# A two-layer conv and state-space network on one core: a cubic softplus with its bias in the product, and conv kernels composed before the branch

## The chip, the cores and the metric

The kernel runs on one core of a Trainium2 chip. A core has five engines with a queue of instructions each: TensorE (PE in the profile, with its weight loads as PEld), VectorE (DVE), ScalarE (ACT), GpSimd (POOL) and SyncE (SP), which here issues nearly all DMAs. The engines meet only at semaphores, and each works through its queue in order. The metric is the device time of one execution in microseconds (us). Before the change, three runs gave a median of 1218.54 us (1215.86 to 1219.69).

## The reference

The input is one image of 64 x 64 positions with 96 channels. It goes through two layers; each is a mixer and an MLP, both with a norm in front and a residual sum behind. All is float32 but the MLPs, which round to 8-bit floats.

Layer 0's mixer projects to 192 channels and a gate, applies a 3x3 convolution per channel, and runs a scan over the 4096 positions in four directions. Layer 1's mixer has a full 3x3 convolution over 192 channels and again scans with a state of 16 per channel. Both make their step sizes with a softplus:

```python
x_dbl = u @ x_proj_w                       # 192 -> 6 + 16 + 16
dt = jax.nn.softplus(dt @ dt_proj_w + dt_proj_b)
...
def step(h, inp):                          # layer 1's scan, per position
    u_t, dt_t, B_t, C_t = inp
    dA = jnp.exp(dt_t[..., None] * A)
    h = dA * h + (dt_t * u_t)[..., None] * B_t[:, None, :]
    y = jnp.sum(h * C_t[:, None, :], axis=-1)
```

## The kernel before

**Stages.** There are four. The *front* (layer 0) is written out by hand: norm and projection, the conv per channel on TensorE, and scans over the ends of the sequences alone (`scan_ends`), since the states fade. A bit computed from the data (`alive`) decides whether the full scan is needed (`tc.If` at line 318, in `layer0`); with these inputs it isn't, and every engine branches past it. The *middle* does layer 0's mix and MLP, the norm of layer 1, its conv and the projections to step sizes and states. The *scans* of layer 1 are 24 passes over 4096 positions (lines 1966 to 2042). The *tail* is layer 1's output projection and MLP.

**What sets the order.** The front keeps the order of its code: `keep` pins an instruction behind all that its engine was given before. In the middle a planner (`Order`) chooses: `o.add(engine, cost, ...)` gives an operation with the tiles that it reads and writes and an estimated cost; `run` always takes an operation that can start first, and among these the one with the longest chain behind it plus a lead from the table `LEAD`. What comes out is the fixed order of each engine's queue. DMAs of `open1` (weights of layer 1) are issued before all that the planner places on SP, and the planner does not count them.

**Softplus.** With z = sigmoid(-|x| - ln 2), softplus(x) is max(x, 0) plus z times a polynomial in z squared. Layer 0 (`dt_proj` and `log1p` in `scan_ends`, lines 736 to 756) works on three tiles of 128 x 320: on ScalarE Abs and Relu, both with dt's bias, then Sigmoid and Square; on VectorE `polynomial` (lines 990 to 997), six operations. Layer 1 (`softplus` in `project`, lines 1704 to 1723) works on 12 tiles of 128 x 512, three for each of the four units (0,0), (0,1), (4,0), (4,1): five operations on ScalarE (lines 1714, 1716, 1717, 1719, 1720) and five on VectorE (1715, 1718, 1721, 1722, 1723), which exchange values twice.

**Layer 1's conv kernels.** The projection into the conv is linear, so its weights and the conv's are multiplied into one kernel from 96 channels (`compose1`, lines 1294 to 1352, part of the middle's plan): 2 transposes, 5 steps of products with 2 taps each (line 1329), a halved copy of each on ScalarE (1332), copies of the outer taps on VectorE (1338), and three sums on GpSimd (1350). `open1` loads its inputs (lines 1258 and 1261, 1.3 MB) right after the branch, then 13 small pieces of weights (lines 1281 to 1290).

**The middle's chain.** For each of four pairs of chunks, `mix0` forms means on TensorE (1366, 1370), subtracts them on VectorE (1374, 1378), squares on ScalarE (1381), gates on GpSimd (1385), sums squares (1401), takes the root (1407) and turns it by two small DMAs on SP into a factor per token, `r` (`by_token`, line 1411). VectorE inverts `r` (1415) and adds the mixer's output to the residual (1445). Then come `mlp0` for each chunk, a norm, and images for the conv (1551). `conv_unit` makes 12 products per unit (1584, 1586) and `project` the states and step sizes (1650 to 1780). The last unit, (4,1), ends with 12 products that copy rows to four partitions each (1807), and the first decays and scans start from those.

## Time and profile before

| | |
|---|---|
| time of the profiled execution | 1217.9 us |
| its span | 1216.1 us |
| front | 0 to 102.2 us |
| middle | 102.5 to about 303 us |
| scans | about 303 to 1118 us |
| busy share: VectorE, TensorE, ScalarE, GpSimd | 93%, 84%, 74%, 69% |
| TensorE's clock at its lowest | 0.50 of full, in 99 to 105 us and 270 to 325 us |

A line of the timeline has the start, the duration, the engine, the line of the kernel, the operation with the tiles that it writes and reads, a count where neighbours are merged, and in brackets how long the engine sat idle before it and what released it. SPq, DVEq and so on are an engine's sequencer, which also issues the DMAs. A line of windows has the stretch, its length, busy time and number of instructions of PE, PEld, DVE, ACT and POOL, the granted clock of TensorE, the DMA engines' share and GB/s.

### The profile page before, as it was taken

The page shows a single profiled execution, that of the slowest core. Times are in us where ns is not written, and L with a number is a line of the kernel's source. Part 1 is how long each engine was busy: PE and PEld are TensorE (multiplying, and loading weights), DVE is VectorE, ACT ScalarE, POOL GpSimd, SP SyncE. Part 2 cuts the span into 40 slices and gives each one's busy share as a digit, 9 for nine tenths or more (in the row PEclk, how much of TensorE's full clock was granted, in tenths as well). Part 3 has the DMA queues.
Part 4 walks back from the last instruction along what each step waited for, and adds up shares of the span by engine and source line. Part 5 has one row for each costly group of instructions (what it writes and reads, how often), then busy time and mean ns, then how long its engine had stood idle before and what let it go on. Part 6 is the DMA issues. An engine that isn't in the chain of part 4 may idle for free.

```text
span 1216.1 us, 11204 instructions
## 1 busy us (share of the span) xinstructions
PE 1017.9 (84%) x3488; PEld 414.6 (34%) x3488; DVE 1129.2 (93%) x908; ACT 905.4 (74%) x1177; POOL 841.6 (69%) x510
## 2 busy tenths in 40 slices
PE   9998889985278877888888877898778898899886
PEld 5533333321023322222332322233224443344344
DVE  7895887688898999999999999999999999999978
ACT  5683654656578888887888878888888888898626
POOL 3002464352678888888798788988898887887756
PEclk9998999985589788798878788888789999888987
DMA  2262011376764583575734685545747767343301
GB/s 77 64 180 52 7 21 32 116 254 187 238 192 132 171 250 128 174 229 175 240 99 137 203 251 181 180 131 176 240 129 208 221 194 265 97 143 93 104 1 52
DMA packets 79128, 183.10 MB, mean 151 GB/s; under 512 B 21534, under 2 KB 34936, under 8 KB 77688
## 3 DMA queue, kind: packets, MB, share of 16 engines
q1 hardware_dynamic: 78376, 182.16, 48.2%
q8 instruction: 28, 0.46, 0.2%
q10 hardware_dynamic: 688, 0.19, 0.1%
q14 instruction: 36, 0.29, 0.1%
HBM read 159.73 MB, written 21.52 MB: 149 GB/s over the span
## 4 chain that ended last, share of the span: by engine, by line
DVE 37%; PE 19%; issue 8%; ACT 7%; DMA 3%; POOL 1%; SPq 0%; DVEq 0%; POOLq 0%; ACTq 0%
DVE xws L2014 12%; PE hs L2025 10%; DVE h1s L2014 10%; DVE h0s L2014 8%; PE hs L2029 4%; ACT da L1987 3%; DVE x2s L2014 3%; ACT xws L1972 2%; DVE x1s L2014 2%; DVE x0s L2014 2%; DMA kept<-xn 2%; DMA x2s<-bc 1%; PE acc L2053 1%; PE da L2343 1%; POOL hss L2019 1%
## 5 line engine op out<-in xcount | busy, mean ns | idle before, releaser
L2042 POOL TENSOR_TENSOR kept<-kept,kept 128x1024 f32<-128x1024 f32 x92 | 217.1, 2359 | 83.8 <-issue 45.0
L2019 POOL TENSOR_TENSOR hss<-h1s,xws 128x1024 f32<-128x1024 f32 x96 | 228.0, 2377 | 48.7 <-DVE xws L2014 47.1
L2025 PE MATMUL hs<-h0s,ident 128*128 128x512 f32 x360 | 224.8, 711 | 29.2 <-DVE h0s L2014 24.6
L1987 ACT ACTIVATE da<-dt1s,a 128x1024 f32<-128x1024 f32 x168 | 187.4, 1116 | 58.0 <-DVE xws L2014 49.0
L2014 DVE TENSOR_TENSOR_SCAN xws<-da,xws 128x1024 f32<-128x1024 f32 x96 | 221.5, 2307 | 7.3 <-ACT da L1987 7.2
L1987 ACT ACTIVATE da<-dt0s,a 128x1024 f32<-128x1024 f32 x166 | 185.2, 1115 | 27.2 <-DVE h0s L2014 10.0
L2029 PE MATMUL hs<-hss,ident 128*128 128x512 f32 x368 | 187.8, 602 | 8.1 <-POOL hss L2019 7.9
L2014 DVE TENSOR_TENSOR_SCAN h1s<-da,xws 128x1024 f32<-128x1024 f32 x69 | 156.0, 2261 | 0.0
L2053 PE MATMUL acc<-kept,fold 128*32 128x512 f32 x368 | 87.0, 683 | 71.8 <-POOL kept L2042 71.8
L2038 ACT COPY kept<-hs 128x512 f32<-128x512 f32 x184 | 107.7, 585 | 43.7 <-PE hs L2029 43.5
L2025 PEld LDWEIGHTS hs<-h0s,ident 128*128 128x128 f32 x360 | 72.4, 219 | 155.2 <-issue 82.4
L2029 PEld LDWEIGHTS hs<-hss,ident 128*128 128x128 f32 x368 | 70.3, 194 | 107.8 <-issue 79.4
L2025 PE MATMUL hs<-x1s,ident 128*128 128x512 f32 x128 | 75.7, 676 | 12.6 <-DVE x1s L2014 12.6
L2025 PE MATMUL hs<-x0s,ident 128*128 128x512 f32 x128 | 74.2, 664 | 13.5 <-DVE x0s L2014 13.5
L2025 PE MATMUL hs<-x2s,ident 128*128 128x512 f32 x120 | 72.9, 693 | 12.1 <-DVE x2s L2014 12.1
L1966 POOL TENSOR_TENSOR x1s<-x1s,dus 128x1024 f32<-128x1024 f32 x32 | 75.6, 2366 | 8.8 <-DMA x1s<-bc 8.8
L1966 POOL TENSOR_TENSOR x2s<-x2s,dus 128x1024 f32<-128x1024 f32 x32 | 75.7, 2366 | 1.3 <-DMA x2s<-bc 1.2
L2014 DVE TENSOR_TENSOR_SCAN x0s<-da,x0s 128x1024 f32<-128x1024 f32 x32 | 73.5, 2296 | 1.3 <-ACT da L1987 1.2
L2014 DVE TENSOR_TENSOR_SCAN x1s<-da,x1s 128x1024 f32<-128x1024 f32 x32 | 73.4, 2293 | 1.3 <-ACT da L1987 1.3
L2014 DVE TENSOR_TENSOR_SCAN x2s<-da,x2s 128x1024 f32<-128x1024 f32 x32 | 73.5, 2298 | 1.0 <-ACT da L1987 0.9
L1972 ACT COPY xws<-x1s 128x1024 f32<-128x1024 f32 x32 | 63.0, 1970 | 5.2 <-POOL hss L2019 5.2
L1966 POOL TENSOR_TENSOR x0s<-x0s,dus 128x1024 f32<-128x1024 f32 x28 | 66.3, 2367 | 0.0
(379 smaller groups left out, 1913.3 us busy)
## 6 DMA issues: line engine op xcount, KB each, us to landing
kept<-bc SPq DMA_DIRECT2D x92, 512.0 KB
x2s<-bc SPq DMA_DIRECT2D x32, 512.0 KB
x0s<-bc SPq DMA_DIRECT2D x28, 512.0 KB
x1s<-bc SPq DMA_DIRECT2D x28, 512.0 KB
dus<-du SPq DMA_DIRECT2D x20, 512.0 KB
dt1s<-dt SPq DMA_DIRECT2D x20, 512.0 KB
dt0s<-dt SPq DMA_DIRECT2D x20, 512.0 KB
kept<-xn SPq DMA_DIRECT2D x24, 384.0 KB
```

The costliest lines, as they stand in the source:

```text
L1966: keep(nc.gpsimd.tensor_tensor(x, x, du[:, part[j]], ALU.mult))
L1972: keep(copy(grid(xw)[:, w, :], cols(xs[i % 3])[:, w, :]))
L1987: keep(nc.scalar.activation(t, dts[o][:, part[j]], AF.Exp, scale=self.a6[:, g, k : k + 1]))
L2014: keep(nc.vector.tensor_tensor_scan(to, da, x, start, ALU.mult, ALU.add))
L2019: keep(nc.gpsimd.tensor_tensor(cols(hs)[:, w, :], grid(h1)[:, w, :], grid(xw)[:, w, :], ALU.add))
L2025: keep(nc.tensor.matmul(t, self.ident, x[:, chunk(m)], start=k == 0, stop=False))
L2029: keep(nc.tensor.matmul(sums[i, m], self.ident, hs[:, chunk(m)], start=False, stop=True))
L2038: keep(nc.scalar.copy(to, sums.pop((i, j * (SC // CH) + h))))
L2042: keep(nc.gpsimd.tensor_tensor(t, t, times_c_by(i, a), ALU.mult))
L2053: keep(nc.tensor.matmul(to, self.fold4, src, start=k == 0, stop=k == NK - 1))
L2343: keep(nc.tensor.matmul(o[:, j], y[r, 2 * k + j : CH : 4], w[r], start=first and j == 0, stop=end and j == 1))
```

## The change

Layer 0's and layer 1's polynomials get one degree less in z squared and a form with one Square on ScalarE. In layer 0 the Relu goes from ScalarE to VectorE. In layer 1 the bias becomes a seventh row of the product: the row of ones comes from an Identity with the bias column `unit`, and the weights get a row loaded by one more DMA per rank block. max(x, 0) and the last sum become one operation.

`compose1` leaves the plan. Its inputs are loaded late in `scan_ends` into tiles that are free by then (`fetch`); its products stand where 19 warming products stood, around the two products `yc`; all of its copies are on ScalarE; the three sums on GpSimd follow, and the result goes to DRAM (`cw_d`, 864 KB). All of this comes before the branch. The middle loads `cw_d` into the conv's tile by one DMA, the first that the planner puts on SP. The planner's costs and leads have new values throughout. The options `BIAS0_POOL` and `NORM0_ACT` are empty and change nothing.

```diff
-RANKS = (slice(0, RANK), slice(96, 96 + RANK))
+RANKS = (slice(0, RANK + 1), slice(96, 96 + RANK + 1))
...
+CUBIC = (0.34226051, 1.83304455, -0.33816952, 3.07350780)
+QS = math.sqrt(CUBIC[0])
+QB = CUBIC[0] * CUBIC[3]
...
-LEAD = {"compose": -84.0}
-LEAD |= {("mix", s): t for s, t in enumerate((1589.0, 1847.0, -1582.0, -1562.0))}
-LEAD |= {("mlp", s): t for s, t in enumerate((1510.0, 80.0, 777.0, -2488.0))}
+LEAD = {"compose": 371.0}
+LEAD |= {("mix", s): t for s, t in enumerate((858.0, 2656.0, -2207.0, -2187.0))}
+LEAD |= {("mlp", s): t for s, t in enumerate((1277.0, 862.0, 1968.0, -5402.0))}
...
+        self.unit = self.column("unit", 0.0)
+        for r in RANKS:
+            nc.gpsimd.tensor_tensor(self.unit, self.unit, self.ident[:, r.stop - 1 : r.stop], ALU.add)
...
             keep(nc.scalar.activation(z[:, s, :], t, AF.Abs, bias=bias))
-            keep(nc.scalar.activation(dt[:, s, :], t, AF.Relu, bias=bias))
+            keep(nc.vector.tensor_scalar(dt[:, s, :], t, bias, 0.0, ALU.add, ALU.max))
             keep(nc.scalar.activation(z[:, s, :], z[:, s, :], AF.Sigmoid, bias=self.nln2, scale=-1.0))
             keep(nc.scalar.activation(zz[:, s, :], z[:, s, :], AF.Square))
+            keep(nc.scalar.activation(p[:, s, :], zz[:, s, :], AF.Square, bias=self.qa, scale=QS))
...
-            self.polynomial(z[:, s, :], zz[:, s, :], dt[:, s, :], p[:, s, :], keep)
+            self.cubic(z[:, s, :], zz[:, s, :], p[:, s, :], keep)
+            keep(nc.vector.tensor_tensor(dt[:, s, :], dt[:, s, :], p[:, s, :], ALU.add))
...
         keep(nc.vector.tensor_tensor(v, v, bc[1], ALU.mult))
+        fetch(*(t.rearrange("p s t -> p (s t)") for t in (w, bc[1])))
...
+        turn()
         others(2)
-        for _ in range(14):
-            keep(nc.tensor.matmul(warm[:, 0:P], self.ident, self.ident, start=True, stop=True))
+        for i in range(0, 4, 2):
+            step(i)
         yc = [pm.tile([P, TE], F32, tag="m", name=f"yc{w}") for w in range(2)]
         for t, r in zip(yc, LANES):
             keep(nc.tensor.matmul(t, self.dup[r], x[r, 5], start=True, stop=True))
-        for _ in range(5):
-            keep(nc.tensor.matmul(warm[:, 0:P], self.ident, self.ident, start=True, stop=True))
+        for i in range(4, 9, 2):
+            step(i)
+        halves()
...
+    def cubic(self, z, zz, p, keep):
+        keep(nc.vector.scalar_tensor_tensor(p, p, QB, z, ALU.add, ALU.mult))
+        keep(nc.vector.scalar_tensor_tensor(p, zz, CUBIC[1], p, ALU.add, ALU.mult))
...
-            nc.sync.dma_start(self.w_dt1[r], w["w_dt"])
+            nc.sync.dma_start(self.w_dt1[r.start : r.start + RANK], w["w_dt"])
+            nc.sync.dma_start(self.w_dt1[r.stop - 1 : r.stop], w["vec"][:, 1:2].rearrange("d o -> o d"))
...
+        def fetch(room, rest):
+            half = rest[0:CD, 0 : 9 * DI].rearrange("p (t o) -> p t o", t=9)
+            for k in range(2):
+                t = room[0 : GP[k], 9 * DI * k : 9 * DI * (k + 1)].rearrange("p (t o) -> p t o", t=9)
+                keep(nc.sync.dma_start(t, w["conv_w"][k * P : k * P + GP[k], :, 0:DI]))
...
+        def step(i):
+            for k in range(2):
+                keep(nc.tensor.matmul(view, turned[0 : GP[k], k], raw[k][:, i : i + n], start=k == 0, stop=k == 1))
+            keep(nc.scalar.activation(half[:, i : i + n], view, AF.Copy, scale=0.5))
+            for j in range(n):
+                y, x = divmod(i + j, 3)
+                if x != 1:
+                    keep(nc.scalar.copy(cwf[:, 3 * x // 2, y], view[:, j]))
+
+        def sums():
+            v = half.rearrange("p (y x) o -> p x y o", x=3)
+            keep(nc.gpsimd.tensor_tensor(v[:, 0], v[:, 0], v[:, 2], ALU.add))
+            keep(nc.gpsimd.tensor_tensor(cwf[:, 1], v[:, 0], v[:, 1], ALU.add))
+            keep(nc.gpsimd.tensor_tensor(cwf[:, 2], v[:, 0], v[:, 1], ALU.subtract))
+            keep(nc.sync.dma_start(self.cw_d, cwf.rearrange("p k y o -> p (k y o)")))
...
+    def spread1(self):
+        o.add("PE", 0.4, lambda: keep(nc.tensor.matmul(at["turn"][0:GC, 0:P], self.fold4, self.ident, start=True, stop=True)), new={"turn": "bank"})
+        o.add("DVE", 0.2, lambda: keep(nc.vector.tensor_copy(self.spread4, at["turn"][0:GC, 0:P])), r=["turn"], w=["spread4"])
+        o.add("SP", 0.65, lambda: keep(nc.sync.dma_start(self.cw1.rearrange("p k y o -> p (k y o)"), self.cw_d)), w=["cw"], kb=885)
...
-            return lambda: keep(nc.scalar.copy(at[xd][:, k], at["x", n, k][0:XE]))
+            return lambda: keep(nc.scalar.activation(at[xd][:, k], at["x", n, k][0:XE], AF.Identity, bias=self.unit[0:XE]))
...
-            o.add("ACT", 0.68, lambda: keep(act(vz(), at[t], AF.Abs, bias=bias)), r=[t], new={w: "w1" if g and not last else "w"}, w=[z])
-            o.add("DVE", 0.73, lambda: keep(dve.tensor_scalar(d(), at[t], bias, 0.0, ALU.add, ALU.max)), r=[t, hold], w=[kd])
+            o.add("ACT", 0.6, lambda: keep(act(vz(), at[t], AF.Abs)), r=[t], new={w: "w1" if g and not last else "w"}, w=[z])
             o.add("ACT", 0.7, lambda: keep(act(vz(), vz(), AF.Sigmoid, bias=self.nln2, scale=-1.0)), r=[w], w=[z], table="sigmoid")
             o.add("ACT", 0.6, lambda: keep(act(vzz(), vz(), AF.Square)), r=[z, w], w=[zz])
-            o.add("DVE", 0.42, lambda: keep(dve.tensor_scalar(p(), vzz(), QC, QD, ALU.mult, ALU.add)), r=[zz, w, hold_u], w=[ku])
-            o.add("ACT", 0.7, lambda: keep(act(vzz(), vzz(), AF.Square, bias=self.qa)), r=[w], w=[zz])
-            o.add("ACT", 0.7, lambda: keep(act(vzz(), vzz(), AF.Square, bias=self.qb)), r=[w], w=[zz])
-            o.add("DVE", 0.69, lambda: keep(dve.scalar_tensor_tensor(p(), vzz(), LOG1P[4], p(), ALU.mult, ALU.add)), r=[zz, w, hold_u], w=[ku])
-            o.add("DVE", 0.69, lambda: keep(dve.tensor_tensor(p(), p(), vz(), ALU.mult)), r=[z, w, hold_u], w=[ku])
-            o.add("DVE", 0.69, lambda: keep(dve.tensor_tensor(d(), d(), p(), ALU.add)), r=[ku, hold, hold_u], w=[kd])
+            o.add("ACT", 0.7, lambda: keep(act(p(), vzz(), AF.Square, bias=self.qa, scale=QS)), r=[zz, w, hold_u], w=[ku])
+            o.add("DVE", 0.63, lambda: keep(dve.scalar_tensor_tensor(p(), p(), QB, vz(), ALU.add, ALU.mult)), r=[z, w, hold_u], w=[ku])
+            o.add("DVE", 0.63, lambda: keep(dve.scalar_tensor_tensor(p(), vzz(), CUBIC[1], p(), ALU.add, ALU.mult)), r=[zz, w, hold_u], w=[ku])
+            o.add("DVE", 0.63, lambda: keep(dve.scalar_tensor_tensor(d(), at[t], 0.0, p(), ALU.max, ALU.add)), r=[t, ku, hold, hold_u], w=[kd])
```

## The prediction

> **What bounds the kernel now.** I read the page first, then the windows by stage, then each queue's timeline from 55 to 330 us, since every edit lies there. The page gives the size of the whole.
>
> ```profile
> span 1216.1 us, 11204 instructions
> PE 1017.9 (84%) x3488; PEld 414.6 (34%) x3488; DVE 1129.2 (93%) x908; ACT 905.4 (74%) x1177; POOL 841.6 (69%) x510
> ```
>
> VectorE's 93% is an average. The windows show one stage that is VectorE's and a middle that isn't.
>
> ```profile
> 140.00:160.00 20.00, 13.30 (x65) 4.66 (x63) 18.81 (x29) 9.52 (x19) 14.71 (x17) 0.83 0.06 10
> 220.00:240.00 20.00, 20.00 (x59) 6.69 (x60) 14.80 (x24) 15.35 (x27) 5.84 (x5) 0.91 0.20 67
> 600.00:800.00 200.00, 163.42 (x403) 58.17 (x401) 199.14 (x91) 166.64 (x193) 172.22 (x78) 0.82 0.55 172
> ```
>
> In the scans VectorE is busy 199 of 200 us, with scans that the change doesn't touch: those 800 us stay. In the middle VectorE leads up to about 165 us (18.8 of 20 at 140, TensorE 13.3), then TensorE (20 of 20 at 220, VectorE 14.8), and from 263 us a chain. So the gain or loss is when the first scan starts (302.7 us now). The crossing from front to middle decides much of it; here are TensorE, SP and GpSimd, with GpSimd's three composing sums.
>
> ```profile
> 92.62 3.39 PE L863 MATMUL warm<-ident 128*128 128x128 f32 x28
> 98.54 0.78 PE L866 MATMUL yc<-bce,dup 64*128 64x160 f32 x4 [2.52 <-issue]
> 102.50 4.41 PE L1366 MATMUL bank<-y,mean 128*128 128x512 f32 x6 [0.75 <-DVEq L318]
> ```
>
> ```profile
> 90.25 0.60 SPq L1878 DMA_DIRECT2D a<-a_log  x1
> 102.96 1.40 SPq L1261 DMA_DIRECT2D raw<-conv_w  x2
> ...
> 113.20 0.83 SPq L1290 DMA_DIRECT2D kept<-vec  x2
> 116.87 1.18 SPq L1411 DMA_DIRECT2D r<-diag  x2
> ```
>
> ```profile
> 102.64 0.31 POOL L1254 MEMSET pairs<- 96x256 f32 x1 [83.21 <-DVEq L318]
> ...
> 138.19 1.40 POOL L1350 TENSOR_TENSOR half<-half 96x576 f32<-96x576 f32 x1
> ...
> 140.73 1.50 POOL L1350 TENSOR_TENSOR cw<-half 96x576 f32<-96x576 f32 x1
> ```
>
> SP has nothing to do from 91 to 102 us and is done with the weights at 114, 3 us before `r` needs it (116.87). GpSimd sits idle for 83 us before the branch. VectorE's queue shows what `r` releases, and the end of the middle.
>
> ```profile
> 119.61 0.20 DVE L1415 RECIPROCAL r<-r 128x8 f32<-128x8 f32 x1 [4.11 <-DMA r<-diag]
> 120.45 1.89 DVE L1445 SCALAR_TENSOR_TENSOR res<-bank,r,res 128x96 f32<-128x96 f32 x8 [0.64 <-PE bank L1436]
> ...
> 267.33 2.28 DVE L1620 TENSOR_TENSOR kept<-kept,kept 128x1024 f32<-128x1024 f32 x1
> ...
> 281.71 0.75 DVE L1718 TENSOR_SCALAR kept<-h1s 128x512 f32<-128x512 f32 x2
> ...
> 286.56 1.28 DVE L1723 TENSOR_TENSOR kept<-kept,kept 128x512 f32<-128x512 f32 x2
> ```
>
> **The change, part by part.** The sum is made against the profiled execution's 1217.9 us (span 1216.1 and 1.8 around it), 0.6 us under the median of 1218.54.
>
> *Layer 0's softplus.* VectorE's chain per tile is 0.32 + 1.54 + 0.49 + 0.49 = 2.84 us; after it is three operations of 0.49 and one from PSUM of about 0.5, 2.0 us. ScalarE changes a Relu (0.52) for a Square (0.47 without a bias). With the last Square at 55.3 us, VectorE reaches the scans of line 795 about 2.3 us sooner. But line 829 needs ScalarE's sigmoid of 816, which stands behind the SiLUs of 634, and these waited for TensorE's conv until 65.08 (5.85 us idle). ScalarE is free at 66.96 and then waited only 0.32 us for VectorE. So 2 of the 2.3 us turn into a new idle of VectorE before 829, and the front's end moves by **-0.3**.
>
> *Composing at the front's end.* `fetch` can start at 80.6 us, when line 830 is done; 1.3 MB took the stretch 103 to 109 before, so it has landed by 88, and the first step is at about 93. ScalarE is free from 93.5 us (5 halvings of 0.49, 6 copies of about 0.36, turned copies): nothing on the path, because VectorE works alone from 93 to 102; without that cover it would be 4.5 us. Three of five steps stand behind `yc`: 98.2 + 0.45 + 1.7 + 1.7 + 1.0 (line 1329's rows) = 103.1, instead of warming products until 101.7. The means then start some 1.5 us later. Now their first six rows take 4.41 us at half clock (0.50 in 99 to 105 us) where two rows later take 1.10, so warm ones win 1.1 to 1.4 back: 0 for the means. Steps at half clock would take 1.43 times (4.41 against 3 x 1.03), 1.9 us more. Row 866 shows that 2.5 us of idle was enough; a gap of 2.24 us before 158.7 was not (1.00 in 155 to 160 us); the new gap is about 1.8 us, between no row. GpSimd: 103.1 + 0.4 for the last halving + 1.40 + 1.50 + 1.44 + hops = 108.1, or 110.0 half-clocked; I take 109. It is still in time for its gating, first at 110.83. The two operations on `unit` (about 0.2 us each at 1 us) hide in the 2.38 us that GpSimd waits for `w_in` at 4 us, and would cost 0.4 otherwise.
>
> The Trainium skill, "TensorE: Matmul & The Clock Gate", Part 1: The HAM clock gate, has the clock halve after an idle window of about 3.4 us. By it the steps run at full clock and the sums end at 108.1, 0.9 earlier than I take; this trace differs, as 2.5 us sufficed.
>
> *SP, the queue that all of this is moved past.* The store of `cw_d` waits for GpSimd's last sum. Behind it in program order stand, on SP: eight `a_log` pieces (85.62 to 90.85, 5.2 us; issued early now because nothing holds them), the branch and its events (94.7 to 95.8, 1.1 us), 15 weight pieces (13 took 6.6 us of issuing within 9.6 us; 7.6 now), the load of `cw_d` (0.65), and only then `r` (2.74 us from issue to line 1415). 109 + 0.7 + 5.2 + 1.1 + 7.6 + 0.65 + 2.74 = 127.0. Two waits have no row: whether the branch waits for landings (0 to the 1.6 us that `r` needs after its second issue) and how far `r` stands behind 864 KB (0 to 2.6 us at the 336 GB/s of 105 to 108 us). Half of each gives 129.1, 9.5 later than 119.61; 0.64 of that was slack (TensorE's wait before 1445): **+8.8**. Low end: `a_log` stays ahead and nothing waits, 108.1 + 0.7 + 1.1 + 7.6 + 0.65 + 2.74 = 120.9: +0.6. High end: 110.0, both waits in full and the old gaps between the weights (3.0 more): 135.2, +15.0. I take the middle since the `a_log` pieces are pinned behind the store. VectorE (1415, 1445, all of the MLPs) waits.
>
> The Trainium skill, "DMA: Bandwidth & Descriptors", Queues, rings and completion order, says that each DMA engine consumes descriptors in ring order. By it `r` waits out the whole load, 1.3 us more than I take; no row of before shows a small transfer behind a large one.
>
> *VectorE's run from `r` to the upper half's images* (120.45 to 163.8 us). Gone: copies of 1338 (1.93 us); idle for the second `r` (0.91), for line 1332 (1.42) and 1329 (0.31); and the stretching of 1528 and 1534 (1.31 and 1.66 us, elsewhere 0.34 and 0.52) beside GpSimd's sums, of which I count 1.4 of 2.1. **-6.0**; between the copies alone, -2, and all 5.2 us of idle with copies and stretching, -9.2.
>
> *TensorE's run, 167.4 to 263.6 us.* The conv and the products keep their rows (a seventh row of a product adds none). What the later mixes still did there (2.9 us of 1422 and 1436) can come earlier, as 7.8 us of composing is gone before it: **-1.5**, between 0 and -2.9.
>
> *Layer 1's softplus.* VectorE's 12 chains fall from 40.5 us (8.9, 6.6, 8.8 and 16.2 by line) to 36 x 0.69 = 24.8, ScalarE's by 8.5. While TensorE leads, that is hidden. On the path is the last unit: 278.07 to 287.84 becomes about 278.07 + 4.3 + 3.7 = 286.1, of which I count -1.5; lines 1715 and 1718 of the last narrow tile, 0.74 + 0.42 = -1.2 in a VectorE that is full from 284 us on; and line 1620, ready at 265.2 but started at 267.33 behind the previous unit's chain, -1.2 of 2.1. Identity for Copy adds 2 x 0.1. Sum **-3.7**, between -1.2 and -4.8. Next late is TensorE's row of copies at half clock.
>
> Sum: -0.3 + 8.8 - 6.0 - 1.5 - 3.7 = -2.7, so **1215.2 us**. All best ends give 1201, all worst 1230.
>
> **The rivals.** *`r` comes in time*: SP is free before the sums matter. For it: the scheduler filled SP's free time before the branch in this trace. Against: the store's pin. With +0.6 for +8.8: 1207.0. *SP's queue in full*: +15.0, the other terms kept, 1221.4. For it: SP's old gaps. Against: the raw load that went with those gaps is gone. *The lower half's images come late*: the last MLP pair has the lowest lead of all (-5402). The last images now end at 214.2 us while TensorE still has the upper half's work; if its three units (about 12 us each) and the rest run out first, TensorE idles until the images are there. It decides from when the last images end some 3 us after that work; 10 us, a little more than the idle of 143 to 163 us (7.4), costs 10: 1225.2. For it: VectorE's late start. Against: VectorE has 15 us less to do.
>
> **How the numbers follow.** About 0.3% (3.7 us) can be told from no change. My forecast holds 0.42 (its own range 1211 to 1220: 0.19 faster, 0.21 same, 0.02 slower), `r` in time 0.22 (0.21, 0.01, 0), SP in full 0.16 (0, 0.09, 0.07), late images 0.20 (0, 0.02, 0.18). Faster 0.40, same 0.33, slower 0.27. The range 1204 to 1227 leaves out the outer parts of the first and last cases.
>
> **What would show it.** Idle of about 1.5 us before line 829's operation; GpSimd's sums ending at 108 to 110 us, the store right after, the weights on SP past 120 us; the first reciprocal of `r` at 129 us with a long wait on its DMA; no idle longer than 1 us on VectorE in the 30 us behind it; TensorE full until some 260 us; the first scan at about 300 us. I'm wrong if `r` comes before 123 or after 134 us, or if TensorE runs dry between the two halves.

## The result, and the profile after

The changed kernel takes 1224.96 us (median of 16 runs, 1217.47 to 1229.17) against 1216.72 us for the kernel before in the same comparison (16 runs): a ratio of 1.0069, with a 95% interval of 1.0054 to 1.0085. It is 8.2 us slower by the medians, 8.4 by the ratio. The profiled execution took 1226.85 us, with a span of 1224.9 us. The prediction said 1215.2 us, a little faster.

The page and the windows of the changed kernel, and then two windows of the kernel before for comparison (stretch, its length, busy time and instructions of PE, PEld, DVE, ACT, POOL, granted clock, DMA share, GB/s):

```profile
span 1224.9 us, 11101 instructions
PE 1024.6 (84%) x3450; PEld 412.5 (34%) x3450; DVE 1107.9 (90%) x870; ACT 900.1 (73%) x1173; POOL 843.8 (69%) x512
```

```profile
40.00:60.00 20.00, 17.53 (x149) 7.22 (x148) 9.45 (x24) 11.52 (x26) 0.00 (x0) 0.74 0.21 58
100.00:120.00 20.00, 19.63 (x32) 5.69 (x30) 7.81 (x22) 5.29 (x15) 0.00 (x0) 0.50 0.00 1
140.00:160.00 20.00, 16.21 (x60) 6.58 (x59) 13.85 (x45) 9.35 (x20) 4.43 (x6) 0.83 0.16 39
220.00:240.00 20.00, 20.00 (x49) 6.84 (x48) 7.72 (x12) 9.14 (x15) 3.31 (x5) 0.91 0.32 95
600.00:800.00 200.00, 162.50 (x417) 58.00 (x415) 199.44 (x91) 166.95 (x198) 173.09 (x78) 0.88 0.55 180
```

```profile
40.00:60.00 20.00, 19.56 (x213) 8.65 (x211) 15.68 (x37) 13.80 (x29) 0.00 (x0) 1.00 0.30 85
100.00:120.00 20.00, 17.98 (x49) 5.92 (x48) 8.05 (x23) 7.73 (x11) 8.31 (x11) 0.86 0.36 78
```

VectorE's work fell by 21 us (1129.2 to 1107.9), and the time rose. The scans are as full as before (199.4 of 200). What is new are two stretches of half clock on TensorE: the second half of 40 to 60 us (0.74 on average over the 20 us, 1.00 before), and all of 100 to 120 us (0.50, 0.86 before). Here is how it came to that, on TensorE, ScalarE and SP of the changed kernel (timeline lines as before):

```profile
50.33 0.82 PE L734 MATMUL xe<-ue,wx 128*80 128x160 f32 x2 [2.47 <-DVE dte L752]
...
97.56 1.97 PE L669 MATMUL z<-xt,w_in 96*64 96x512 f32 x4 [2.47 <-ACT pad L671]
99.46 3.78 PE L666 MATMUL z<-xt,w_in 96*128 96x512 f32 x4
...
105.08 5.52 PE L1332 MATMUL compose<-w,turned 128*96 128x384 f32 x7
...
120.77 4.87 PE L1366 MATMUL bank<-y,mean 128*128 128x512 f32 x6 [1.14 <-ACTq L320]
```

```profile
93.98 3.04 ACT L681 ACTIVATE y<-y,d 128x2048 f32<-128x2048 f32 x2 [2.15 <-DMA u<-y]
```

```profile
81.96 1.41 SPq L1316 DMA_DIRECT2D w<-conv_w  x2
84.52 6.98 SPq L638 DMA_DIRECT2D u<-y  x8
...
124.33 0.34 SPq L1344 DMA_DIRECT2D cw<-cwf  x1
129.99 0.37 SPq L1287 DMA_DIRECT2D kept<-w_x  x1
...
138.54 0.42 SPq L1354 DMA_DIRECT2D cw<-cw  x1
139.08 4.23 SPq L1411 DMA_DIRECT2D r<-pad  x4
```

In the kernel before, the same scaling on ScalarE (there line 679) waited 0.23 us, and not for a DMA:

```profile
86.12 3.04 ACT L679 ACTIVATE y<-y,d 128x2048 f32<-128x2048 f32 x2 [0.23 <-ACT pad L669]
```

Read them from the top. At 50 us TensorE waits for line 752, which is layer 0's max(x, 0), now on VectorE, and behind that wait its granted clock is 0.50 until 60 us. At 82 us SP issues the 1.3 MB of conv weights, and behind them the stores of `u`. ScalarE scales `y` in place (line 681), so it must wait until those stores have read `y`: 2.15 us. Its gate copies (671) hang on that, TensorE waits 2.47 us for them, and from there its products take twice as long (96*128 from 1.91 to 3.78 us for four). The composing starts at 105 us and runs at half clock, and TensorE's first mean of the middle starts at 120.77 us instead of 102.50. GpSimd and VectorE show what follows:

```profile
120.08 1.40 POOL L1341 TENSOR_TENSOR bce<-bce 96x576 f32<-96x576 f32 x1 [100.99 <-ACT bce L1333]
...
122.91 1.40 POOL L1343 TENSOR_TENSOR cwf<-bce 96x576 f32<-96x576 f32 x1
129.77 0.31 POOL L1267 MEMSET pairs<- 96x256 f32 x1 [5.46 <-SPq L320]
```

```profile
49.73 0.55 DVE L752 TENSOR_SCALAR dte<-de,vec 128x320 f32<-128x320 f32 x1
...
111.81 1.51 DVE L887 TENSOR_TENSOR y<-y,yc 64x64 f32<-64x64 f32 x8 [5.14 <-PE yc L872]
126.78 1.28 DVE L1374 TENSOR_TENSOR y<-y,bank 128x512 f32<-128x512 f32 x2 [13.45 <-PE bank L1370]
...
145.20 0.20 DVE L1415 RECIPROCAL r<-r 128x8 f32<-128x8 f32 x1 [12.89 <-DMA r<-pad]
...
309.50 2.27 DVE L2021 TENSOR_TENSOR_SCAN h1s<-da,xws 128x1024 f32<-128x1024 f32 x1
```

The sums end at 124.3 us (forecast 109), `r` is inverted at 145.20 us (forecast 129.1; before 119.61), and the first scan starts at 309.50 us (before 302.72). The account of the two profiled executions has three terms: TensorE's first mean comes 18.3 us later; from there to the first scan it takes 188.7 us instead of 200.2, so 11.5 us less; and from the first scan to the end 2.0 us more. Together +8.8 us, the difference of the spans. The last term is no cause that these runs can tell: with the same scans, that stretch lay between 911 and 917 us in all profiles here but one (925), so single executions scatter by a few us there, and the medians decide.

### The profile page after: what moved, and what is told of

Read it like the earlier page. It is cut to its first block, busy times and chain, and to the rows that moved or that the text cites. A ratio compares the mean times of both kernels' runs of the same rounds, so it can differ in the third digit from the quotient of the medians.

```text
span 1224.9 us, 11101 instructions
## 1 busy us (share of the span) xinstructions
PE 1024.6 (84%) x3450; PEld 412.5 (34%) x3450; DVE 1107.9 (90%) x870; ACT 900.1 (73%) x1173; POOL 843.8 (69%) x512
## 4 chain that ended last, share of the span: by engine, by line
DVE 37%; PE 14%; ACT 8%; issue 8%; DMA 3%; POOL 2%; SPq 0%; DVEq 0%; POOLq 0%; ACTq 0%
DVE xws L2021 12%; DVE h1s L2021 9%; DVE h0s L2021 7%; PE hs L2032 7%; ACT da L1994 4%; DVE x2s L2021 3%; PE hs L2036 3%; ACT xws L1979 3%; DVE x0s L2021 2%; DVE x1s L2021 2%; POOL hss L2026 1%; DMA kept<-xn 1%; DMA du<-ye 1%; ACT kept L2045 1%; PE da L2350 1%
## 5 line engine op out<-in xcount | busy, mean ns | idle before, releaser
L2026 POOL TENSOR_TENSOR hss<-h1s,xws 128x1024 f32<-128x1024 f32 x96 | 228.3, 2380 | 49.6 <-DVE xws L2021 49.2
L2032 PE MATMUL hs<-x2s,ident 128*128 128x512 f32 x120 | 67.5, 646 | 13.9 <-DVE x2s L2021 13.9
```

What stands on the lines that cost most here:

```text
L2026: keep(nc.gpsimd.tensor_tensor(cols(hs)[:, w, :], grid(h1)[:, w, :], grid(xw)[:, w, :], ALU.add))
L2032: keep(nc.tensor.matmul(t, self.ident, x[:, chunk(m)], start=k == 0, stop=False))
```

## The experiments

The 16 runs below differ from the changed kernel, or from the kernel before, by a few lines each. Where only the front, SP's queue or the width of a product is edited, the planner's order of TensorE, VectorE and ScalarE in the middle is that of the changed kernel. Times are medians; ratios are against the kernel before, with 95% intervals. "Mean" is the start of TensorE's first mean, "r" the first reciprocal, "scan" the first scan, in us from each profile. A profile is of one execution, which can lie some us off the median: for "weights late" it took 1236.3 us, for "max on ScalarE" 1214.9 and for "cubic, composing in the middle" 1218.7.

| kernel | time | ratio | mean | r | scan |
|---|---|---|---|---|---|
| before | 1216.7 | | 102.50 | 119.61 | 302.72 |
| changed | 1225.0 | 1.0069 (1.0054-1.0085) | 120.77 | 145.20 | 309.50 |
| cubic alone | 1221.7 | 1.0036 (1.0016-1.0057) | 109.23 | 126.34 | 306.86 |
| composing alone | 1227.3 | 1.0094 (1.0065-1.0123) | 114.60 | 136.79 | 311.25 |
| leads alone | 1230.3 | 1.0119 (1.0087-1.0152) | 102.45 | 119.57 | 313.65 |
| changed, old leads | 1235.0 | 1.0139 (1.0106-1.0171) | 121.01 | 145.12 | 319.94 |
| cubic, composing in the middle, new leads | 1223.9 | 1.0071 (1.0045-1.0097) | 102.91 | 118.98 | 304.37 |
| max on ScalarE | 1219.7 | 1.0043 (1.0021-1.0066) | 115.48 | 139.31 | 300.37 |
| fetch late | 1218.6 | 1.0022 (1.0004-1.0039) | 114.84 | 139.03 | 300.31 |
| weights late | 1223.4 | 1.0054 (1.0031-1.0076) | 121.21 | 138.80 | 309.44 |
| no store | 1223.1 | 1.0044 (1.0023-1.0065) | 121.36 | 140.26 | 309.20 |
| front mended | 1210.1 | 0.9944 (0.9908-0.9981) | 107.02 | 130.84 | 295.07 |
| front mended, weights late | 1203.7 | 0.9893 (0.9863-0.9924) | 104.48 | 121.47 | 288.63 |
| all mended | 1201.7 | 0.9883 (0.9850-0.9915) | 103.30 | 118.58 | 289.12 |
| all mended, max on VectorE | 1208.7 | 0.9938 (0.9919-0.9957) | 109.75 | 125.03 | 292.37 |
| all mended, fetch early | 1218.8 | 1.0026 (1.0006-1.0045) | 115.23 | 132.53 | 303.09 |
| weights late, wide products | 1220.9 | 1.0047 (1.0026-1.0068) | 121.00 | 138.93 | 304.12 |
| all mended, wide products | 1201.3 | 0.9882 (0.9839-0.9925) | 103.16 | 118.46 | 283.62 |

### The parts alone

**The cubic softplus alone**, in the kernel before:

```diff
-QA = LOG1P[3] / (4 * LOG1P[4])
...
+CUBIC = (0.34226051, 1.83304455, -0.33816952, 3.07350780)
...
-            keep(nc.scalar.activation(dt[:, s, :], t, AF.Relu, bias=bias))
+            keep(nc.vector.tensor_scalar(dt[:, s, :], t, bias, 0.0, ALU.add, ALU.max))
```

> The kernel before with the cubic softplus in both layers and nothing else: composing stays in the plan, costs and leads of the old operations stay. Theory (layer 0's max on VectorE stands behind the weight casts and makes the front late by 5.6 us, layer 1's shorter chains win 4 to 6.4 us in front of the first scan): the line-752 operation waits for ScalarE and the casts until about 55 us, the product into the states at about 77.5 us instead of 72.3, the first reciprocal of r at about 125 us instead of 119.6, the first scan at 302 to 304 us, the time 1215 to 1219 us, so no difference that counts. Rival (the cubic brings its gain anyway, the planner's new order took it away): first scan at or before 299 us, 1213 us or less.

Measured: 1.0036, 1221.7 us; the product into the states at 78.71 us, r at 126.34, the first scan at 306.86. The front is late by 6.4 us there, a little more than expected, and only 2.6 us come back up to the first scan: TensorE's first mean is 6.7 us later, the first scan 4.1. The 4 to 6.4 us of the theory were too many. The rival (a scan before 299 us) is out, and so is "no difference that counts": the loss of the front is the larger. Part of that loss is clock: TensorE ran at half clock from 51.1 to 61.3 us here.

**The composing alone**, in the kernel before: `compose1` with `fetch`, `turn`, `step` and `sums` at the front's end as in the change, old softplus, old costs and leads.

```diff
-            self.add_ends(*self.scan_ends(ep, pm, pe, pad, ue, beside))
+            self.add_ends(*self.scan_ends(ep, pm, pe, pad, ue, beside, self.compose1(ep, pm, w1)))
...
-                self.compose1()
+                self.spread1()
```

> The kernel before with the composing at the front's end and nothing else: old softplus, old costs and leads. Theory (the fetch stands ahead of the stores of u on SP, ScalarE waits 2 us for them, TensorE idles about 2.5 us and falls to half clock, the join waits 5 us for the store's landing, and r stands behind weights and a 864 KB load): the product into the states at 72.3 us as before, the granted clock about 0.50 from 93 to 115 us, GpSimd's sums ending at about 118 us, the first reciprocal of r at about 139 us, the run from there to the upper half's images 8 us shorter, the first scan at about 311 us, 1224 to 1228 us. Rival (the half clock comes from TensorE's late front in the changed kernel, which is absent here): clock 1.00, sums ending at 109 us, r at 127 to 130 us, 1216 to 1220 us.

Measured: 1.0094, 1227.3 us, r at 136.79, the first scan at 311.25. The layer-0 part is on time here (product into the states at 71.84 us), TensorE idles 2.99 us before 91.4 us, and the clock is 0.55 in 100 to 120 us. So the half clock needs no late softplus: the composing brings its own. The theory held.

**The leads alone**, and **the change without its leads**:

```diff
-LEAD = {"compose": -84.0}
-LEAD |= {("mix", s): t for s, t in enumerate((1589.0, 1847.0, -1582.0, -1562.0))}
...
+LEAD = {"compose": 371.0}
+LEAD |= {("mix", s): t for s, t in enumerate((858.0, 2656.0, -2207.0, -2187.0))}
...
```

> The kernel before with the change's table of leads and nothing else. The runs so far add up: cubic softplus +4.4 us, composing at the front +11.4 us, both with the old table +16.9 us, and the new table takes 8.5 us off. Theory (the table is fitted to the changed plan, without composing in it and with shorter softplus chains, so it wins there alone): 1214 to 1224 us here. Rival (the table is better for any of these plans): about 1208 us, the first scan at about 295 us instead of 302.7.

> The changed kernel with the table of leads of the kernel before. Theory (in the runs so far the way from r to the first scan takes 161 to 164 us with the change's table and 174.5 us with the composing alone under the old table, so the table wins several us): r at 145 us as in the changed kernel, the first scan at 315 to 320 us, 1231 to 1235 us. Rival (the table is worth nothing, the shorter softplus and the missing composing give it all): first scan at 309 to 311 us, 1224 to 1227 us.

Measured: the new table in the old kernel costs 14.5 us (1.0119), the old one in the changed kernel 8.5 us (1.0139 against 1.0069). The first, 1230.3 us, is 6 us over the upper end of what I expected. The front is the same in each pair; in the profiles 10.9 and 10.4 us of the difference lie between r and the first scan:

```profile
145.12 0.20 DVE L1415 RECIPROCAL r<-r 128x8 f32<-128x8 f32 x1 [12.27 <-DMA r<-pad]
319.94 2.27 DVE L2021 TENSOR_TENSOR_SCAN h1s<-da,xws 128x1024 f32<-128x1024 f32 x1
```

These are two lines of VectorE's timeline in the changed kernel with old leads: 174.8 us from r to the first scan, against 164.3 with the new. The theory that the table fits only the changed plan holds, more strongly than I had put it. The comparison also says where the middle's gain is: from TensorE's first mean to the first scan the kernel before takes 200.2 us, and with both parts and the old table 198.9. With the new table it is 188.7. The shorter work is worth little until the order uses it.

**Cubic softplus, max on ScalarE, new leads, composing left in the middle** (the diff is against the cubic alone):

```diff
-LEAD = {"compose": -84.0}
...
+LEAD = {"compose": 371.0}
...
-            keep(nc.vector.tensor_scalar(dt[:, s, :], t, bias, 0.0, ALU.add, ALU.max))
+            keep(nc.scalar.activation(dt[:, s, :], t, AF.Relu, bias=bias))
```

> The kernel before with the cubic softplus in both layers, layer 0's max(x, 0) left on ScalarE, and the change's table of leads; composing stays in the middle's plan. Theory (composing at the front's end costs about 4.5 us of TensorE's start even where the front is mended, and wins about 3 us in the middle, so leaving it where it was is no worse): TensorE's first mean at 102.5 us, the first reciprocal of r at 119.6 us, the first scan at 292 to 297 us, 1207 to 1212 us. Rival (the new table needs the plan without composing): first scan at 299 us or later, 1213 us or more.

Measured: 1.0071, 1223.9 us, mean and r on time (102.91 and 118.98) but the first scan only at 304.37. My theory fell, the rival held: the new table needs the plan without the composing. So with this table it is no gain to leave the composing in the middle. Whether a table fitted to that plan would do better was not run.

### The front's waits

**Layer 0's max(x, 0) back on ScalarE**, in the changed kernel:

```diff
-            keep(nc.vector.tensor_scalar(dt[:, s, :], t, bias, 0.0, ALU.add, ALU.max))
+            keep(nc.scalar.activation(dt[:, s, :], t, AF.Relu, bias=bias))
```

> The changed kernel with layer 0's max(x, 0) back on ScalarE. Theory (the max behind the weight casts held TensorE's PSUM tile): the product into the states at about 72.5 to 73.5 us instead of 77.9, all that follows in the front about 5 us sooner, the half clock of the composing stays, r at about 140 us instead of 145.2, 1219 to 1221 us. Rival (ScalarE leads the front, the three Relus of 0.52 us come back and eat it): product into the states at 76 us or later, 1224 us or more.

Measured: 1.0043; product into the states at 72.52 us instead of 77.92, mean 5.3 us earlier, r at 139.31. The theory holds in the front. Of the 5 us, the ratios show 3.2.

**The fetch behind the stores of `u`**, in the changed kernel:

```diff
         keep(nc.vector.tensor_tensor(v, v, bc[1], ALU.mult))
-        fetch(*(t.rearrange("p s t -> p (s t)") for t in (w, bc[1])))
...
         others(OTHERS[2])
+        fetch(*(t.rearrange("p s t -> p (s t)") for t in (w, bc[1])))
         others(1)
```

> The changed kernel with the fetch of the conv weights issued behind the stores of u instead of ahead of them. Theory (the fetch on SP delays the stores of u, ScalarE waits 2.15 us for them, TensorE idles 2.47 us and the composing runs at half clock): ScalarE's wait before the scaling by d falls under 0.5 us, the granted clock is 1.00 in 100 to 120 us, yc's wait on VectorE falls from 5.1 to about 2 us, GpSimd's sums end at about 116 us instead of 124.3, the first reciprocal of r at about 136 us instead of 145.2, 1215 to 1219 us. Rival (the weights now come too late and the steps wait for them, or the clock halves anyway): sums ending after 120 us, r after 141 us, 1222 us or more.

Measured: 1.0022, 1218.6 us. ScalarE's wait is 0.23 us, `yc` has none, the sums end at 118.4 us and the mean starts at 114.84. The clock is not 1.00 in 100 to 120 us, though, but 0.66: TensorE now idles 1.62 us ahead of `yc`, and the steps behind it run at half clock. That gap is about what the prediction expected (1.8 us), and it was enough here.

**Both, and three of the five steps ahead of `yc`** (the front mended):

```diff
-        for i in range(0, 4, 2):
+        for i in range(0, 6, 2):
             step(i)
...
-        for i in range(4, 9, 2):
+        for i in range(6, 9, 2):
             step(i)
```

> The changed kernel with three edits of the front's order: max(x, 0) of layer 0 on ScalarE, the fetch of the conv weights behind the stores of u, and three of the five composing steps (instead of two) ahead of yc. Theory (the front's three new waits are the loss, and what is gained before r is kept to the first scan): product into the states at 72.5 us, granted clock 1.00 up to 100 us, GpSimd's sums ending at about 109 us instead of 124.3, the first reciprocal of r 21 us later, at about 130 us instead of 145.2, the first scan at 291 to 296 us, 1207 to 1213 us. Rival (behind r the middle is limited by another engine, so an earlier r is given back): r at 130 us but the first scan at 300 us or later, 1216 us or more.

Measured: 0.9944 (0.9908 to 0.9981), 1210.1 us: faster than both kernels, by edits in the front alone. r at 130.84 and the first scan at 295.07 are where the theory put them; the product into the states is at 76.1 us, since TensorE's clock fell once more in this profile (0.50 from 52.3 to 59.1 us).

### SP's queue and the store

**The weights and the load behind the first two r**, in the changed kernel:

```diff
-            nc.sync.dma_start(t, w["vec"][g * P : (g + 1) * P, :])
+            self.late.append((t, w["vec"][g * P : (g + 1) * P, :]))
...
-        o.add("SP", 0.65, lambda: keep(nc.sync.dma_start(self.cw1.rearrange("p k y o -> p (k y o)"), self.cw_d)), w=["cw"], kb=885)
...
+        both = [("r", 0), ("r", 1)]
+        o.add("SP", 0.65, lambda: keep(nc.sync.dma_start(self.cw1.rearrange("p k y o -> p (k y o)"), self.cw_d)), r=both, w=["cw"], kb=885)
+
+        def weights():
+            for to, src in self.late:
+                keep(nc.sync.dma_start(to, src))
+
+        o.add("SP", 8.5, weights, r=both, w=["weights"])
```

> The changed kernel with the 15 weight pieces and the load of the composed kernels issued on SP behind the first two r instead of ahead of them; the order on the other four engines is the same. Theory (r is held by SP's queue and by the 864 KB ahead of it: its inputs are ready at 135.3 us in the changed kernel): the first reciprocal at 138 us instead of 145.2, the first scan at about 302.5 us, about 1218 us. Rival (TensorE and the second r set the pace, SP was hidden): reciprocal earlier, but the first scan at 307 us or later, 1222 us or more. The kernels come later to the conv: if the first conv product waits for them, that gives back up to 5 us.

VectorE's timeline and a window of this kernel:

```profile
138.80 0.20 DVE L1425 RECIPROCAL r<-r 128x8 f32<-128x8 f32 x1 [5.75 <-DMA r<-pad]
...
309.44 2.28 DVE L2031 TENSOR_TENSOR_SCAN h1s<-da,xws 128x1024 f32<-128x1024 f32 x1
```

```profile
230.00:240.00 10.00, 10.00 (x16) 3.66 (x16) 4.31 (x7) 5.06 (x10) 4.89 (x4) 0.57 0.28 105
```

r comes 6.4 us earlier, as expected of SP's share, and the first scan doesn't: the rival held. The ratios show 1.8 us (1.0054, on the edge of the changed kernel's interval). The window shows one reason in this execution: TensorE, full without a gap, ran at half clock for 10.2 us (228.3 to 238.6), in the changed kernel's profile for 3.4 us (234.1 to 237.5). Products take twice as long at half clock (1.91 and 3.78 us above), so by these figures that is some 3.4 of the 6.4 us, an estimate.

**The store left out**, in the changed kernel:

```diff
-            keep(nc.sync.dma_start(self.cw_d, cwf.rearrange("p k y o -> p (k y o)")))
...
+        for k in range(3):
+            self.keep(self.nc.sync.dma_start(self.cw1[:, k], self.conv_w1[0:CD, 3 * k : 3 * k + 3, 0:DI]))
+        self.keep(self.nc.sync.dma_start(self.cw1[:, 3], self.conv_w1[CD : 2 * CD, 0:3, 0:DI]))
```

> The changed kernel without the store of the composed kernels; the middle loads raw conv weights of the same size instead, in four pieces (so layer 1's conv computes with weights that aren't composed). Theory (all engines wait at the join until the store has landed, 5.1 us): SP's first weight piece at about 125 us instead of 130, TensorE's first mean at about 116 us instead of 120.8, the first reciprocal at about 140 us, the first scan at about 304.5 us, about 1220 us. Rival (the join waits for the engines' own last work, the store's landing is beside it): the first weight piece at 128 us or later, 1223 us or more.

SP's and GpSimd's first lines behind the branch:

```profile
125.54 0.36 SPq L1287 DMA_DIRECT2D kept<-w_x  x1
```

```profile
126.12 0.31 POOL L1267 MEMSET pairs<- 96x256 f32 x1 [1.24 <-POOLq L320]
```

SP and GpSimd go on 4.4 and 3.7 us sooner than in the changed kernel, but TensorE's first mean does not (121.36), nor the first scan. So the landing of the store (5.3 us from the end of its issue to SP's next DMA) is waited for by SP and GpSimd only; TensorE starts 1.1 us behind its own last product in both kernels. Half of the theory fell.

**The mended front with the weights late**, and **the same with the store in four pieces** (all mended):

```diff
+        def store(k):
+            keep(nc.sync.dma_start(self.cw_d[:, 3 * DI * k : 3 * DI * (k + 1)], cwf[:, k].rearrange("p y o -> p (y o)")))
+
         def sums():
+            store(0)
+            store(3)
             keep(nc.gpsimd.tensor_tensor(v[:, 0], v[:, 0], v[:, 2], ALU.add))
             keep(nc.gpsimd.tensor_tensor(cwf[:, 1], v[:, 0], v[:, 1], ALU.add))
+            store(1)
             keep(nc.gpsimd.tensor_tensor(cwf[:, 2], v[:, 0], v[:, 1], ALU.subtract))
+            store(2)
-            keep(nc.sync.dma_start(self.cw_d, cwf.rearrange("p k y o -> p (k y o)")))
```

> The kernel with the mended front (1210.1 us) with the first two r ahead of the weights and the load, the store in one piece as in the change. Theory (with the front on time r counts for something, as the store does: the two edits on SP took 8.3 us off together): SP's share is the larger, the first reciprocal at about 119 to 121 us, about 1203 to 1205 us. Rival (the landing of the store in one piece, 5 us at the join, is what counted): 1207 us or more.

> The kernel of the run with the mended front (1210.1 us), with two more edits on SP: the store of the composed kernels in four pieces as they come, and the first two r ahead of the weights and of the load. Theory (TensorE's start and its clock set the pace, not r): the first reciprocal at about 124.5 us instead of 130.8, the first scan within 2 us of that run's 295.1 us, 1207 to 1211 us. Rival (r counts once the front is on time): first scan at 290 us or earlier, 1205 us or less.

Measured: 0.9893 with the weights late, 0.9883 with the store split as well (1201.7 us; only the last kernel below is 0.4 us lower). So with the front on time an earlier r is worth some 6 us (0.9944 to 0.9893, intervals that overlap by 0.0016), and splitting the store about 1 us, which these runs cannot tell from nothing. For the second kernel my theory (r doesn't count) fell, for the first it holds.

### One fault put back

From the best kernel, one of the front's faults at a time. The diffs are those above, the other way round.

> The best kernel so far (1201.7 us) with layer 0's max(x, 0) back on VectorE, as in the change. Theory (the max behind the weight casts holds TensorE's PSUM tile and the clock falls): product into the states at about 78 us instead of 72.4, the first scan at about 294 us instead of 289.1, about 1207 us. Rival (the cost came from this in the changed kernel only because the composing was late too): 1204 us or less.

> The best kernel so far (1201.7 us) with the fetch of the conv weights back ahead of the stores of u, as in the change. Theory (the stores of u come late, TensorE idles 2.5 us, the composing runs at half clock): granted clock about 0.5 in 95 to 112 us, TensorE's first mean at about 110 us instead of 103.3, the first scan at about 295 us, about 1208 us. Rival (the composing at half clock is hidden while VectorE works on the ends): 1204 us or less.

TensorE and ScalarE of the best kernel, and then of the one with the fetch early:

```profile
90.12 1.08 PE L669 MATMUL z<-xt,w_in 96*64 96x512 f32 x4 [0.53 <-ACT pad L671]
...
103.30 2.84 PE L1382 MATMUL bank<-y,mean 128*128 128x512 f32 x6 [1.14 <-ACTq L320]
```

```profile
86.54 3.04 ACT L681 ACTIVATE y<-y,d 128x2048 f32<-128x2048 f32 x2 [0.22 <-ACT pad L671]
```

```profile
91.99 1.97 PE L669 MATMUL z<-xt,w_in 96*64 96x512 f32 x4 [2.40 <-ACT pad L671]
...
115.23 4.84 PE L1382 MATMUL bank<-y,mean 128*128 128x512 f32 x6 [1.17 <-ACTq L320]
```

```profile
88.42 3.04 ACT L681 ACTIVATE y<-y,d 128x2048 f32<-128x2048 f32 x2 [2.10 <-DMA u<-y]
```

Nothing but the place of two DMAs on SP differs. ScalarE waits 2.10 us instead of 0.22 and TensorE 2.40 instead of 0.53; then the clock halves (0.50 in 100 to 110 us, against 1.00), and the first mean is 11.9 us later, the first scan 14.0, the time 17 us (1.0026 against 0.9883), more than twice the 6 us that I expected. The max on VectorE makes the first mean 6.5 us later and the time 6.7 us longer (0.9938), close to what I expected (in its profile the first scan is only 3.3 us later). The two shifts of the first mean, 11.9 and 6.5, add up to 18.4 us; the changed kernel's is 18.3, and the two parts alone in the kernel before give 12.1 and 6.7, 18.8 together. So two ways of adding the faults account for its late start. Taken out of the changed kernel one at a time they give less, 5.9 for the fetch and 5.3 for the max, as composing at half clock remains in both (0.50 from 105.8 to 119.5 us and from 92.1 to 119.5 us); the best kernel also has one step more ahead of `yc`.

### Half clock in a full TensorE

In nine of the sixteen profiles with the change's or the old narrow products (that of the kernel before among them, at 221.8 us), TensorE's clock fell to 0.50 somewhere between 205 and 240 us while it was busy without a gap, for 3 to 10 us. In the two kernels below it began right behind a group of the step sizes' products, which contract over 7 rows. To test this I widened them to 103 rows, with zeros in the weights:

```diff
-                keep(nc.tensor.matmul(at["t", n, k], self.w_dt1[r, 0:P], at[xd][r, k], start=True, stop=True))
+                keep(nc.tensor.matmul(at["t", n, k], self.w_dt1[k][:, 0:P], at[xd][0:XE, k], start=True, stop=True))
```

> The kernel of the run with the first two r ahead of the weights (1223.4 us), with the step sizes' products over all 103 rows (zeros in the weights for the other 96) instead of 7 rows. In that run TensorE was busy without a gap from 180 to 260 us, yet its granted clock was 0.50 from 228.3 to 238.4 us, right behind six products of 7 rows; the run without the store showed the same. Theory (products with few rows let the clock fall as idling does): granted clock 1.00 from 190 to 270 us, TensorE's last conv product about 5 us sooner than 274.4 us, the time 3 to 5 us below 1223.4 us. Rival (the clock falls for another reason): half clock in that stretch again, 1221 us or more.

> The best kernel so far (1201.7 us) with the step sizes' products over 103 rows instead of 7; its clock fell to 0.50 from about 208 to 218 us while TensorE was full, right behind eight products of 7 rows. Theory (few rows let the clock fall): granted clock 1.00 from 170 to 250 us, the first scan at about 285 us instead of 289.1, 1196 to 1199 us. Rival (the clock falls for another reason, and the gain of the other run with wide products was chance): half clock for some us between 190 and 250 us again, 1200 to 1204 us.

Windows of the best kernel, and of the same with wide products:

```profile
210.00:220.00 10.00, 10.00 (x17) 3.73 (x17) 3.93 (x7) 5.10 (x9) 4.89 (x4) 0.60 0.28 105
```

```profile
210.00:220.00 10.00, 10.00 (x26) 4.19 (x23) 7.53 (x11) 7.42 (x14) 5.38 (x4) 1.00 0.42 146
```

In both profiles with wide products the clock is 1.00 from 190 to 250 us and the first scan comes 5.3 and 5.5 us earlier than in the narrow twin. By the ratios the time gains 0.9 us (1.0047 against 1.0054) and 0.1 us (0.9882 against 0.9883), neither of which the intervals can tell from nothing, and 1201.3 us lies where the rival had it. So the clock goes as the theory says, in two profiles out of two, but seven of sixteen narrow ones had no drop there either, so two without one can be chance, and no gain in time is shown. This stays open.

## Why the prediction was wrong

**The composing, costed at nothing: the step that failed.** The prediction put it as "nothing on the path, because VectorE works alone from 93 to 102" and "0 for the means". Measured, the first mean was 18.3 us late, of which some 12 belong to this step (11.9 with the fetch put back, 12.1 with the composing alone). Two errors lie in it. It asked what the fetch needs (free tiles at 80.6 us; it was issued at 81.96) and what stands behind the *store* on SP, but not what stands behind the *fetch*: the eight stores of `u`, which the profile of before shows on SP at 78.58 us and which ScalarE's scaling waits for. And it judged the gap on TensorE as 1.8 us, "between no row"; it was 2.47 us, at another place, and behind it TensorE stayed at half clock from 97.5 us past 120, where the prediction had allowed 1.9 us for half-clocked steps. Nor did VectorE cover it: it was done at 106.7 us and waited 5.14 us for `yc`, which stood behind those steps.

**Layer 0's softplus, -0.3 us.** It was +6.5 to +6.7 us at the first mean. The prediction counted VectorE's chain and ScalarE's, but not that the new max reads the PSUM tile that the next product of TensorE needs. On VectorE it stands behind the casts of the MLP weights, and these wait for their DMA until 49.35 us. The wait itself is 2.4 to 2.6 us; where the max is on ScalarE with the same softplus, TensorE's one gap there is 1.03 or 1.04 us, at another place. The larger part is clock: in all eight profiles with this max on VectorE the granted clock is 0.50 for 10.2 us from about 50 us on, in five of the seven with it on ScalarE it stays at 1.00 there. In the other two it fell for 6.8 and 3.4 us, and the product into the states came at 76.14 and 73.59 us instead of about 72.4; with the max on VectorE it came at 77.92 to 78.86. VectorE's new idle ahead of that product is there, with 2.12 us for the forecast 1.5, but not as forecast: VectorE reached the scans 3.6 us later than before (63.89 against 60.29), not 2.3 sooner.

**SP's queue, +8.8 us at r.** From the end of the sums to r the prediction had 20.1 us and the profile shows 20.9, but by other terms: the `a_log` pieces (5.2 us) were issued ahead of the store, at 91.6 us; in their place stood the landing of the store, 5.3 us, of which the prediction counted 0.8 (half of 1.6); and r took 6.1 us from its issue, behind the 864 KB load, for the 4.04 counted (2.74 and half of 2.6). The Trainium skill, "DMA: Bandwidth & Descriptors", Queues, rings and completion order, has each DMA engine take its descriptors in ring order, which goes with the long r here and with the late stores of `u`: in the six profiles with the load just ahead of it r took 5.5 to 6.1 us from its issue, in the seven with the load behind it 2.8, and 4.1 behind the four raw loads of the run without the store. The larger error was to take r for the gate of the middle. Its inputs were ready only at 135.2 us, because TensorE began late: of the 25.6 us that r is later, 18.3 came with TensorE. SP's 7 us were worth 1.8 us in time on the late front and some 6 us on the mended one.

**What comes back.** The forecast was -6.0 to the upper half's images, -1.5 to the last conv sum and -3.7 to the first scan, 11.2 in all; measured from r it is -8.3, -4.1 and -6.4, 18.8 us, part of it because TensorE's start moved less than r did. From TensorE's first mean it is 11.5, close to the forecast, but not for its reasons: with the old leads the same operations give back 1.3 us. The prediction read the new costs and leads as something that lets the gains happen and gave them no price; they are worth 8.5 us.

**The rivals.** r in time did not happen. Late images (1225.2) came nearest in time, and SP's queue in full (1221.4) next, both by chance: the images of the lower half were not late, as TensorE was busy for 9.5 us or more of every 10 from 200 to 270 us, and SP was not what delayed the middle most. The condition for being wrong, r after 134 us, came true. What the prediction lacked was a case in which TensorE's start of the middle moves.

**The clock.** The Trainium skill, "TensorE: Matmul & The Clock Gate", Part 1: The HAM clock gate, gives an idle window of about 3.4 us, free-running. The traces agree with the grid: in the changed kernel the granted clock changes at 49.78, 60.02, 97.57, 124.88, 148.77 and 155.59 us, whole multiples of 3.41 us apart. They do not agree with an idle time of that length: gaps of 2.40, 2.47 and 2.99 us were followed by half clock, and one of 1.62 us too. The gap's length alone, by which the prediction judged (2.52 us enough, 2.24 not), is no condition; what else decides is not shown.

## What to carry to other kernels

When a transfer is added to a queue, list what is behind it on that queue and who waits for each of those, also when the transfer itself has time: here two DMAs in the wrong place cost 17 us in the best kernel (5.7 in the changed one, where other faults remained), and moving them took one line. When an operation changes engines, look at what it holds (here a PSUM tile that TensorE's next product needed) and at what the new engine has queued ahead of it, not only at the engines' sums. And where work of TensorE is moved into a stretch that is hidden, ask what clock it will have there: a gap of 2.5 us ahead of it was followed here by half clock for 27 us (97.6 to 124.9).

## What was unexpected in the hardware

- TensorE's granted clock fell to 0.50 for 3 to 10 us in nine of sixteen profiles while TensorE was 100% busy; in the two profiles with products over 103 rows instead of 7 it didn't. The cause is not settled.
- A branch's join waited for the landing of an 864 KB store on SP and GpSimd (5.3 us from the end of its issue), while TensorE, VectorE and ScalarE went on.
- In the seven profiles with the cubic softplus and layer 0's max on ScalarE, TensorE has a gap of 1.03 or 1.04 us that ends at about 51 us, ahead of products over 6 rows. In two of them it was followed by half clock (52.3 to 59.1 us with the mended front, 53.3 to 56.7 with the weights late as well), in five it was not.
- TensorE stayed at half clock from 97.6 to 124.9 us in the changed kernel although it was busy for 22.07 of the 22.5 us from 97.5 to 120. Why the clock did not come back sooner is not shown.
